# Projections of two sequences together in the last attention of an eight-layer kernel, and inverse square roots by bits and Newton's steps

## The chip, the core and the metric

The kernel runs on one core of a Trainium2 chip. A core has five engines, each with its own instruction queue worked off in order: TensorE (PE, matmuls, with weight loads shown as PEld), VectorE (DVE), ScalarE (ACT), GpSimd (POOL) and SyncE (SP, which only starts transfers). They meet through semaphores. The metric is the device time of one execution in microseconds. The kernel before took 2527.54 us, the median of three runs between 2524.89 and 2529.49.

## The reference

Eight sequences of 256 tokens with 256 features go through eight layers, an attention and a feed-forward in turn, four times; after each layer the input is added and a layer norm follows. The change lies in the seventh layer (a differential attention) and in the very last norm of the eighth (a mixture of 32 experts, four per token). Cut to what matters:

```python
def L3_attn(x):                        # 16 heads, 4 key/value heads, D = 16
    q = rope(x @ Wq); k = rope(x @ Wk); v = x @ Wv
    scores = softmax(causal(q k^T / sqrt(D)))        # two maps per head
    diff = softmax(causal(scores[0] - lam * scores[1]))
    att = diff @ v
    att = att * rsqrt(mean(att * att, -1) + 1e-8) * rms_w
    return (att * (1 - lam_init)) @ Wo

x = layernorm(x + L3_attn(x))
x = layernorm(x + L3_ffn(x))           # softmax over 32 experts, top 4
```

A layer norm here is (x - mean) / sqrt(var + 1e-5).

## The kernel before, in words

The tokens stay on chip: X[b] holds sequence b with tokens on the partitions, xT[k] holds blocks of two sequences transposed (512 columns), which is what matmuls need. PSUM is eight banks of 128x512 f32, handed out by `ps(tag)`: two each for the tags t, a, s and o, in turn.

`attn3` (from L553) is software-pipelined by hand. Within it the order on PE, DVE, ACT and POOL is exactly the order in which the Python code issues instructions; no planner moves them. SP's order is planned by the framework, in this stage and in the next. A **unit** is one sequence b, one half qc of its queries (128 of them) and a group of heads: for qc = 0 there are two units of 128 keys with four score maps each per slot, for qc = 1 four units of 256 keys with two maps. So a sequence has six units, and the loop at the end of `attn3` runs 48 + 3 rounds. I call the rounds of a sequence r0 to r5; r0 and r1 have a unit with qc = 0. Round n does, in this order:

- `factors` of unit n-1: a reciprocal of the softmax sums (DVE, L672), then on POOL a causal select, the factor c in two small products (L682, L683), and another select
- `scores` of unit n: matmuls into four banks, two a and two s (PE, L642), a masking matmul (L655), then row maxima (DVE, L659), then exponentials with sums (ACT, L662)
- `values` of unit n-3: matmuls of the probabilities with V into a bank of tag o (L739), and when a half is complete a copy to oS (L118 or L120, DVE and ACT in turn)
- one step of the projection of the next sequence, then the first half of `differences` of unit n-1: the differences (DVE, L696), their maximum (L700), and on POOL a small product (L701) and the shifted differences v (L704)
- one more projection step (two in r0 and r1), then one step of `finish` of an earlier sequence (the queue `ends`)
- the second half of `differences`
- `turned` of unit n-2: transposes on PE into two banks of tag t (L721), then exponentials on ACT (L723)

A **projection step** (`project`, L596 and L600) is two matmuls of 256 columns into a bank of tag t and a DVE multiplication by a rotary table out of it; twelve of them make q and k of one sequence, and a thirteenth makes V (L616, copied out at L620). All of sequence 0 is projected ahead of the loop.

**finish** (L749 on) normalizes a sequence in six steps: transposes of oS, division by the softmax sums and squares; mean squares (L773) and their inverse root by Ln and Exp on ACT (L780, L781) and one Newton step on POOL (L782 to L785), then the scaling of att (L788); transposes (L795) and a copy aT (L799); the output matmul (L804), the residual (L164) and `moments`; the normed rows; and the transposes for the next layer. Its steps begin in r3 of the following sequence, one per round.

`moments` (L176) takes means and variances on DVE and calls `rsqrt` (L141), which computes (var + eps) to the power -0.5 with two POOL instructions (L146, L147).

When sequence 3 is finished, the sort of the first group of tokens for the experts starts between the rounds (the queue `others`), and then POOL issues 32 indirect transfers that scatter the tokens to sorted rows (L954), three per round.

`ffn3` then runs the expert tiles of group 0, between which the rest of `attn3` (the finish of sequence 7) and the sort of group 1 are stepped; then the tiles of group 1; then `ffn3_combine` of group 1: per half sequence POOL issues four indirect gathers (L2048), DVE adds them up weighted (L2054), and after two halves `moments`, the norm and the output transfer (L197) follow.

Of the kernel before, what the change touches and what calls it, by code (L numbers as in the profile page):

```python
# [10 lines left out]
F32 = mybir.dt.float32  # L11
# [28 lines left out]
class Model:  # L40
# [135 lines left out]
    def moments(self, r):  # L176
# [8 lines left out]
        self.rsqrt(rstd, mv[:, :, 1], 1.0, LN_EPS)  # L185
# [367 lines left out]
    def attn3(self, w, act, keep, start=False, beside=None):  # L553
# [29 lines left out]
        qTs, kTs, oT, oSs = {}, {}, {}, {}  # L583

        def project(b):

            if start:
                self.transpose_x(b)
            xT = self.xT[b // 2][:, :, (b % 2) * T : (b % 2 + 1) * T]
            qT = act.tile([P, 8, T], F32, tag="qT", name="qT")  # L590
            kT = act.tile([P, 2, T], F32, tag="kT", name="kT")

            def turn(out, wt, i, tab):
                ps = self.ps("t")[:, :T]
                for c in range(2):
                    nc.tensor.matmul(  # L596
                        ps, wt[:, c, i * P : (i + 1) * P], xT[:, c, :],
                        start=(c == 0), stop=(c == 1),
                    )
                nc.vector.tensor_tensor(out, ps, tab, ALU.mult)  # L600

            for a in range(2):
                k = kT[:, a, :]
                turn(k, w["wk"], 2 * a, w["ck"][:, a, :])
                yield
                x = act.tile([P, T], F32, tag="kh", name="kh", bufs=1)
                turn(x, w["wk"], 2 * a + 1, w["sk"][:, a, :])
                nc.gpsimd.tensor_tensor(k, k, x, ALU.add)
                yield
            for j in range(8):  # L610
                turn(qT[:, j, :], w["wq"], j, w["tq"][:, j % 2, :])
                yield
            ps = self.ps("t")[:, :128].rearrange("p (t n) -> p t n", t=2)
            for t in range(2):
                for c in range(2):
                    nc.tensor.matmul(  # L616
                        ps[:, t, :], xT[:, c, t * P : (t + 1) * P], w["wv"][:, c, :],
                        start=(c == 0), stop=(c == 1),
                    )
            nc.vector.tensor_copy(  # L620
                Vs[b % 2][:, :, :, 0:16], ps.rearrange("p t (s d) -> p t s d", s=4)
            )
            qTs[b], kTs[b] = qT, kT
            yield
# [1668 lines left out]
```

## Time and profile before

| what | us |
|---|---|
| median of three runs | 2527.54 |
| profiled execution, its own time | 2512.97 |
| its span | 2511.2 |
| setup and projections of sequence 0 | 1741 to 1759 |
| rounds of attn3 | 1759 to 2216 |
| expert tiles of group 0 | 2216 to 2346 |
| expert tiles of group 1 | 2346 to 2455 |
| gathers and last norms | 2455 to 2511 |

Over the whole span PE is busy 2192.5 us (87%), DVE 1431.1 (57%), ACT 1047.5 (42%) and POOL 916.9 (37%). These shares are means over stages with different limits. Where a stretch of the trace is listed, each row has busy time and number of instructions of each engine in it, then the mean granted TensorE clock, the share of time in which the transfer engines were busy, and GB/s. A list of waits names the waiting engine, tile and line, then the releasing one, the total in us, how often, and the longest. In a timeline an idle time stands in brackets with the instruction that ended it. Successive DVE instructions overlap a little: a 128x512 instruction that shows 0.68 lets the next start after 0.60, a 128x256 one that shows 0.41 after 0.33.

### The profile page before, as it was taken

What the parts mean: (1) busy time and instruction counts of PE and PEld (TensorE: products, weight loads), DVE (VectorE), ACT (ScalarE), POOL (GpSimd) and SP (SyncE); (2) the same over time, 40 slices, a digit from 0 to 9 for tenths busy, and PEclk for the clock granted to TensorE, in tenths of its full rate; (3) what the DMA queues carried; (4) which work ended last, traced back from release to release, by engine and by line L of the source; (5) the groups of instructions that cost most, each with busy time, mean ns of one, the idle gap of its engine ahead of it and who ended that gap; (6) DMA issues with size and microseconds to landing.
All of it is one profiled execution on the core that took longest, in us unless ns stands there. A gap on an engine that the chain in (4) does not pass through costs nothing. (4 is left out here: it accounts for less than half of the span.)

```text
span 2511.2 us, 36255 instructions
## 1 busy us (share of the span) xinstructions
PE 2192.5 (87%) x11960; PEld 1494.2 (60%) x12016; DVE 1431.1 (57%) x3593; ACT 1047.5 (42%) x3005; POOL 916.9 (37%) x1725
## 2 busy tenths in 40 slices
PE   7998899999999999999999999998877777678990
PEld 4554697756666666666664465555555554457780
DVE  4556486754544543544465454565888878645463
ACT  1334365453544544544432112221766755644450
POOL 1222443343433323333312321000566557833555
PEclk9999999999999999999999999999999978789995
DMA  5000411100000100000260011002000000145663
GB/s 160 1 1 1 165 44 40 59 5 4 3 3 8 47 1 1 1 1 1 74 206 1 1 51 52 1 0 103 1 2 1 1 1 26 41 125 172 213 212 96
DMA packets 92309, 120.76 MB, mean 48 GB/s; under 512 B 9757, under 2 KB 79582, under 8 KB 91102
## 3 DMA queue, kind: packets, MB, share of 16 engines
q1 hardware_dynamic: 82270, 95.75, 11.8%
q0 software_dynamic: 8192, 21.11, 2.8%
q8 instruction: 100, 1.64, 0.3%
q10 hardware_dynamic: 1664, 1.57, 0.2%
q14 instruction: 83, 0.68, 0.1%
HBM read 67.53 MB, written 50.88 MB: 47 GB/s over the span
## 5 line engine op out<-in xcount | busy, mean ns | idle before, releaser
L1391 POOL TENSOR_SCALAR p<-p,rs 128x128 f32<-128x128 f32 (+1 forms) x256 | 104.2, 425 | 294.7 <-DVE rs L1389 290.4
L1381 ACT ACTIVATE p<-ps_s,nm,rq 128x128 f32<-128x128 f32 (+1 forms) x256 | 128.0, 507 | 152.2 <-DVE nm L1379 152.2
L1309 ACT ACTIVATE sq<-ps_a 128x512 f32<-128x512 f32 x126 | 76.0, 603 | 227.2 <-PE ps_a L1301 226.9
L146 POOL TENSOR_SCALAR rsq<-bnmv 128x2 f32<-128x2 f32 x64 | 13.6, 212 | 377.5 <-DVE bnmv L184 369.9
L662 ACT ACTIVATE e<-ps_a,nm 128x128 f32<-128x128 f32 (+1 forms) x256 | 105.9, 435 | 107.7 <-DVE nm L659 98.4
L1310 DVE TENSOR_REDUCE ssk<-sq 128x4 f32<-128x512 f32 x64 | 43.8, 686 | 172.9 <-ACT sq L1309 172.9
L704 POOL TENSOR_SCALAR v<-e,r,nmd 128x128 f32<-128x128 f32 (+1 forms) x256 | 134.6, 537 | 10.0
L1301 PE MATMUL ps_a<-w_a_wq,xT 128*128 128x512 f32 x256 | 122.3, 600 | 12.4 <-DVE k L1323 9.4
L721 PE MATMUL ps_t<-ident,v 128*128 128x128 f32 x384 | 69.2, 317 | 61.7 <-DVE qT L600 29.4
L1301 PE MATMUL ps_a<-w_a_wv,xT 128*128 128x512 f32 x256 | 120.6, 593 | 1.0 <-ACT q L1334 1.0
L1981 PE MATMUL ps_a<-w_f_gup,xTg 128*128 x504 | 111.5, 345 | 11.4 <-DVE xTg L1975 6.9
L696 DVE SCALAR_TENSOR_TENSOR e<-e,c 128x128 f32<-128x128 f32 (+1 forms) x256 | 105.1, 460 | 25.5 <-POOL c L683 25.3
L1310 DVE TENSOR_REDUCE ssq<-sq 128x4 f32<-128x512 f32 x64 | 43.9, 686 | 129.8 <-ACT sq L1309 129.8
L1301 PE MATMUL ps_a<-w_a_wk,xT 128*128 128x512 f32 x248 | 116.5, 593 | 0.0
L1429 PE MATMUL ps_o<-w_a_wo,attT 128*128 128x256 f32 x512 | 111.8, 379 | 0.0
L662 ACT ACTIVATE e<-ps_s,nm 128x128 f32<-128x128 f32 (+1 forms) x256 | 106.8, 452 | 0.0
L1429 PEld LDWEIGHTS ps_o<-w_a_wo,attT 128*128 128x128 f32 x512 | 96.7, 190 | 12.8
L1163 DVE SCALAR_TENSOR_TENSOR yg<-ps_t,xg,yg 128x128 f32<-128x128 f32 x266 | 93.1, 350 | 12.7 <-PE ps_t L1152 3.9
L1368 PE MATMUL ps_s<-kT,qT 128*128 128x256 f32 (+1 forms) x512 | 100.3, 329 | 0.0
L721 PEld LDWEIGHTS ps_t<-ident,v 128*128 128x128 f32 x384 | 50.2, 163 | 81.4 <-issue 31.4
L1415 PE MATMUL ps_o<-pT,V 128*128 128x256 f32 x256 | 79.5, 392 | 19.2 <-ACT pT L120 19.2
L1981 PEld LDWEIGHTS ps_a<-w_f_gup,xTg 128*128 128x128 f32 x504 | 82.4, 197 | 22.2 <-ACT yg L2011 10.6
(410 smaller groups left out, 6041.7 us busy)
## 6 DMA issues: line engine op xcount, KB each, us to landing
rows<-zero SPq DMA_DIRECT2D x42, 384.0 KB, 4.5
xg<-rows SPq DMA_DIRECT2D x42, 384.0 KB, 5.1
outs<-yg SPq DMA_DIRECT2D x42, 384.0 KB, 3.7
w_f_gup<-in_f_gup SPq DMA_DIRECT2D x8, 768.0 KB, 8.6
w_f_w<-in_f_w SPq DMA_DIRECT2D x8, 512.0 KB, 6.3
w_f_down<-in_f_down SPq DMA_DIRECT2D x8, 384.0 KB, 8.3
w_f_up<-in_f_up SPq DMA_DIRECT2D x5, 512.0 KB, 7.3
lrows<-zero SPq DMA_DIRECT2D x12, 204.0 KB, 5.7
```

The source lines that it names most:

```text
L662: nc.scalar.activation(e[:, s, j * nk : (j + 1) * nk], sc[s][:, j, :], AF.Exp, bias=nm[:, s, j : j + 1], scale=1.0, accum_out=sums[:, s, j ...
L696: nc.vector.scalar_tensor_tensor(d[:, s, h, :], u.e[:, s, h, 1, :], u.c[:, s, h : h + 1], d[:, s, h, :], ALU.mult, ALU.add,)
L704: nc.gpsimd.tensor_scalar(u.v[:, s, h, :], d[:, s, h, :], u.r[:, s, h, 0:1], nm[:, s, h : h + 1], ALU.mult, ALU.add,)
L721: nc.tensor.transpose(ps[:, s, c, :], x, self.ident)
L1163: nc.vector.scalar_tensor_tensor(acc[j], y, c, acc[j], ALU.mult, ALU.add)
L1301: nc.tensor.matmul(ps, self.xt(u.b, t, c), w[which][:, c, u.cols], start=(c == 0), stop=(c == 1),)
L1310: nc.vector.tensor_reduce(out, sq, AX.X, ALU.add)
L1368: nc.tensor.matmul(sc[:, j, :], u.qT[:, h0 + j, qc * P : (qc + 1) * P], u.kT[:, h0 + j, 0:nk], start=(j == 0), stop=False,)
L1381: nc.scalar.activation(u.p[qc][:, h0 + j, :], sc[:, j, :], AF.Exp, bias=nm[:, j : j + 1], scale=r[:, j : j + 1], accum_out=u.sums[qc][:, h ...
L1391: nc.gpsimd.tensor_scalar(u.p[qc][:, j, :], u.p[qc][:, j, :], ri[:, j : j + 1], 1.0, ALU.mult, ALU.mult,)
L1429: nc.tensor.matmul(y[:, t, :], attTs[b][:, h, t * P : (t + 1) * P], w["wo"][:, h, :], start=(h == 0), stop=(h == 15),)
L1981: nc.tensor.matmul(ps, xT[j][:, c, :], w["gup"][:, bass.ds(er[j], 1), c, :].rearrange("p o f -> p (o f)"), start=(c == 0), stop=(c == 1),)
```

## The change

In `attn3`:

- Projections are made for a block of two sequences, so a part has 512 columns instead of 256, and there are twelve parts per block. Block 0 (sequences 0 and 1) is projected ahead of the loop; the parts of block k + 1 are issued one per round in the twelve rounds of block k. The two banks of tag o are taken once: `bank_o` for the values, `bank_x` for the parts and for V. The DVE instruction that empties a part comes at the start of the next round, ahead of the row maxima. V is still made per sequence, in r2, and the part of r2 follows at the end of that round.
- The shifted differences v are written over the differences in e instead of to a tile of their own; qT becomes four tiles per block.
- The inverse root in `finish`: two DVE instructions make a first guess from the bits, one more forms the mean, and three Newton steps of four POOL instructions each replace the Ln, the Exp and the one Newton step.
- `finish` has twelve steps instead of six, and two are taken per round, so that it still lasts six rounds.

In `ffn3`: the leftover of `attn3` is stepped at two of three tiles instead of one of three; and the norms of group 1, except the last, take their root by bits and Newton's steps on DVE instead of POOL's power.

```diff
+    def rsqrt_bits(self, out, v, eng):
+        half = ... tag="nm" ...
+        self.nc.vector.tensor_scalar(half, v.bitcast(I32), 1, None, ALU.arith_shift_right)
+        self.nc.vector.tensor_scalar(
+            out.bitcast(I32), half, -1.0, float(0x5F3759DF), ALU.mult, ALU.add)
+        for _ in range(3):
+            eng.tensor_tensor(t, out, out, ALU.mult)
+            eng.tensor_tensor(t, t, v, ALU.mult)
+            eng.tensor_scalar(t, t, -0.5, 1.5, ALU.mult, ALU.add)
+            eng.tensor_tensor(out, out, t, ALU.mult)
...
+        bank_o, bank_x = self.ps("o"), self.ps("o")
+        def project(blk, banks):
+            def part(to, wt, i, tab):
+                def turn():
+                    ps.append(banks())
+                    for c in range(2):
+                        nc.tensor.matmul(ps[0], wt[:, c, i * P : (i + 1) * P], xT[:, c, :], ...)
+                def out():
+                    nc.vector.tensor_tensor(to..., ps[0]..., tab..., ALU.mult)
+                    if wt is w["wk"] and i % 2:
+                        nc.gpsimd.tensor_tensor(k, k, to, ALU.add)
...
-                u.v = act.tile([P, 4, u.nh, u.nk], F32, tag="v", name="v", bufs=3)
+                u.v = d
...
             yield
+            yield
             ms = self.small.tile([P, 2, 16], F32, tag="ms", name="ms")
...
-            g.tensor_scalar(ms, ms, 1.0 / 16.0, 1e-8, ALU.mult, ALU.add)
+            nc.vector.tensor_scalar(ms, ms, 1.0 / 16.0, 1e-8, ALU.mult, ALU.add)
+            nc.vector.tensor_scalar(half, ms.bitcast(I32), 1, None, ALU.arith_shift_right)
-            nc.scalar.activation(rr, ms, AF.Ln)
-            nc.scalar.activation(rr, rr, AF.Exp, scale=-0.5)
-            g.tensor_tensor(ms, ms, rr, ALU.mult)
-            g.tensor_tensor(ms, ms, rr, ALU.mult)
-            g.tensor_scalar(ms, ms, -0.5, 1.5, ALU.mult, ALU.add)
-            g.tensor_tensor(rr, rr, ms, ALU.mult)
+            nc.vector.tensor_scalar(
+                rr.bitcast(I32), half, -1.0, float(0x5F3759DF), ALU.mult, ALU.add)
+            yield
+            for i in range(3):
+                g.tensor_tensor(t, rr, rr, ALU.mult)
+                g.tensor_tensor(t, t, ms, ALU.mult)
+                g.tensor_scalar(t, t, -0.5, 1.5, ALU.mult, ALU.add)
+                g.tensor_tensor(rr, rr, t, ALU.mult)
+                if i < 2:
+                    yield
...
+            if out:
+                out()
...
-            step(projections)
+            v = project_v(n // 6 + 1) if n % 6 == 2 and n // 6 + 1 < NB else None
+            if v:
+                v[0]()
+            elif parts:
+                f, out = parts.pop(0)
+                f()
             halves = last.differences() if last else iter(())
             next(halves, None)
-            step(projections, 2 if u and u.qc == 0 else 1)
             step(ends)
+            if v:
+                v[1]()
...
+            step(ends)
+            if v and parts:
+                f, out = parts.pop(0)
+                f()
...
-                m = self.moments(rs[b])
+                m = self.moments(rs[b], g == 1 and i < 2 * n - 1)
...
-            if len(left) > 1 and j % 3 != 2:
+            if len(left) > 1 and j % 3 == 0:
```

## The prediction

> **What bounds the kernel now.** I read the busy times by stretch first, one row per sequence of the seventh layer (1854 to 1907 is sequence 2).
>
> ```profile
> core 0: us, PE busy (x) PEld busy (x) DVE busy (x) ACT busy (x) POOL busy (x), PEclk, DMA share, GB/s
> 1741.00:1759.00 18.00, 17.00 (x98) 13.92 (x99) 7.39 (x20) 0.59 (x1) 2.05 (x3) 0.81 0.80 326
> ...
> 1854.00:1907.00 53.00, 40.18 (x369) 27.54 (x360) 45.31 (x102) 37.46 (x147) 33.51 (x83) 0.97 0.01 1
> 1907.00:1961.00 54.00, 42.73 (x364) 29.15 (x360) 45.60 (x103) 37.05 (x146) 33.29 (x81) 0.91 0.00 1
> ...
> 2146.00:2216.00 70.00, 46.81 (x346) 28.75 (x346) 46.98 (x105) 39.70 (x151) 55.37 (x115) 0.76 0.10 35
> ...
> 2455.00:2511.00 56.00, 0.00 (x0) 0.00 (x0) 22.24 (x56) 0.00 (x0) 34.80 (x40) 0.50 0.32 94
> ```
>
> In sequences 2 to 4 DVE is busy 45 of 53 us: it is the bound, with 8 us of stalls. In sequence 7 POOL has taken over, because it also issues the scatter. In the tail only POOL and DVE work. The list of waits (1760 to 2200) names the stalls.
>
> ```profile
> POOL nmd L701 <- DVE nmd L700: 91.0, 53, 8.1
> ...
> PE ps_t L721 <- DVE qT L600: 29.4, 23, 3.1
> ...
> DVE e L696 <- POOL c L683: 16.8, 14, 2.9
> DVE nm L659 <- PE ps_a L655: 16.8, 17, 2.3
> ...
> POOL ms L782 <- ACT rr L781: 13.7, 7, 2.0
> ...
> DVE V L620 <- PE ps_t L616: 11.9, 6, 5.2
> ...
> DVE res L164 <- PE ps_t L804: 8.8, 5, 1.8
> ```
>
> The largest is harmless: POOL waits for the engine that bounds. The fourth to the last are what DVE itself loses. PE waits for DVE to empty t banks and so starts the next scores late (29.4, then 16.8 for DVE). POOL waits for ACT's root and then gives c late. The timeline shows this in r4 and r5 of sequence 2, ACT first:
>
> ```profile
> 1895.45 1.28 ACT L780 ACT_TABLE_LOAD   x1
> ...
> 1901.33 0.29 DVE L620 COPY V<-ps_t 128x128 f32<-128x128 f32 x1 [1.43 <-PE ps_t L616]
> 1903.48 1.04 DVE L696 SCALAR_TENSOR_TENSOR e<-e,c 128x256 f32<-128x256 f32 x2 [1.86 <-POOL c L683]
> ```
>
> Two table loads and two small activations (3.0 us) delay ACT's exponentials, hence the values, V and c: DVE loses 1.43 + 1.86 us. The tail's timeline shows POOL's queue:
>
> ```profile
> 2467.90 0.94 POOL L2048 DMA_INDIRECT yk<-outs,r_slots  x1 [0.30 <-issue]
> 2469.14 0.94 POOL L2048 DMA_INDIRECT yk<-outs,r_slots  x1 [0.30 <-issue]
> 2470.16 0.19 POOL L146 TENSOR_SCALAR rsq<-bnmv 128x2 f32<-128x2 f32 x1
> 2470.43 0.72 POOL L147 TENSOR_TENSOR rstd<-rsq,nhalf 128x2 f32<-128x2 f32 x1
> 2471.34 1.17 POOL L2048 DMA_INDIRECT yk<-outs,r_slots  x1 [0.19 <-issue]
> ```
>
> **Ahead of the loop.** A part of 256 columns takes 0.865 us once the clock is up (DVE empties one each 0.86 us), twelve 10.4; the observed twelve took 13.0, since the first four came at up to 1.7 us. The clock's 2.6 us extra is what must be scaled or not. The row alone suggests doubling all: +13.0. The Trainium skill (TensorE: Matmul & The Clock Gate, Part 1) says that the warm-up is a span of time of about 3.4 us and not a number of matmuls; then only 12 x 0.865 doubles: **+10.4 us**. I take that; the four slow parts fill one such span and a bit. DVE's emptying (0.60 each) is hidden behind PE's 1.73. If that cover failed, it would cost 12 x 0.6 more.
>
> **Rounds of a full sequence.** I add DVE's work between one round's first maximum and the next's, by the starts of the rows: maxima 4 x 0.60 = 2.4; differences and maximum 2.95 for a qc = 1 unit, 3.8 for qc = 0; reciprocal 0.11 or 0.16; a part 0.60 (the 128x512 residual out of a t bank, L164, shows 0.69 and occupies 0.60), so six per sequence cost 3.6 where twelve at 0.33 cost 4.0.
>
> - r0: 2.4 + 2.95 + 0.16 + 0.6 = 6.1, plus a wait for POOL. A Newton instruction is priced by L782 to L785 (0.22 to 0.25, next start 0.33 later), so a step is 1.3. At the end of r5 POOL does step 2 (1.3), the product and v of the second half (1.4), step 3 (1.3) and the scaling (1.2), all behind the first half's v; it ends 5.1 after DVE's last maximum. The select and c (0.9) follow, at 6.0, while DVE needs c after 3.1. DVE waits 2.9: r0 is 9.0.
> - r1: 2.4 + 3.8 + residual and moments 1.8 + normed rows 0.7 + 0.76 = 9.5. Behind scores on PE stand values 0.6, part 1.73 and output matmul 1.73, 4.1 in all; DVE asks at 4.3, so no wait.
> - r2: DVE 7.7. PE is longer: V must be copied out (5.5), the X transposes free a t bank at about 5.6, turned ends at 6.2, the part moved to the end takes 1.73, the scores 1.3: 9.2.
> - r3: 2.4 + 2.95 + divisions 1.2 + 0.7 = 7.3; turned waits for both t banks: 7.4.
> - r4: 2.4 + 0.3 + 2.95 + mean squares 0.65 + three small DVE instructions at 0.2 (a 128x32 integer one, L901, shows 0.18) + 0.7 = 7.6.
> - r5: 6.1 plus 0.5, because POOL's step 1 brings c at 3.6 instead of 3.1: 6.6.
>
> The sum is 49.3. Before, sequences 2, 3 and 4 took 52.9, 54.1 and 53.4 by their first reciprocals. So -4.2 each, **-12.5 us**. The gain is in r5 (9.3 to 6.6) and r3; r1 and r2 get longer (8.4 to 9.5, 8.5 to 9.2). For c and Newton's steps the unknown is POOL's pace: without any waits in r0 and r5 a sequence saves 7.6, with steps at twice the price nothing (below).
>
> **The other sequences.** Sequence 1 took 49.8; without the residual and X transposes in its first rounds r0, r1 and r2 follow the cycle exponentials 5.5, scores 1.5, first maximum 0.7, signals (7.85, 7.85, 8.2), then as above: 45.5, **-4.3**. Sequence 0 has no finish: the first wait for scores now covers the part, **-2**. Sequence 5 holds the sort, whose work stays; -3.6 by the same rounds. In 6 and 7 POOL is the bound: a qc = 0 round with scatter is 9.6, qc = 1 8.1. Newton's twelve instructions (4.0) take the place of five plus the 1.95 wait for ACT (3.6), and the sum of the two k additions (1.5) leaves sequence 6. Table loads no longer delay V (5.2 once) and c. **-2.5 and -2**. In the drain and the expert tiles the finish of sequence 7 takes tiles 1 to 17 instead of 2 to 17: nothing. Its table loads (2229.7 to 2234.1) lay inside a 6.9 us PE wait for a transfer. SP's queue has as many transfers; the gathers of rows and the stores of outs swap places here and there, priced 0, within 3 either way: around 2347 PE waits 3.6 us behind such a store. v in e costs nothing: e is read by turned two rounds later and written again three rounds later, so that cover holds by one PE queue position.
>
> **The tail.** 32 gathers at a cadence of 1.25 us take 38.8 from first start to last; observed are 42.5, so three roots cost 1.23 each. They leave POOL; the last stays. DVE gets fifteen dependent small instructions, about 0.19 each as L184 (0.18): 2.9 in place of the 2.64 wait. Per eight gathers (10 us) DVE has 8 x 0.51 + 1.25 + 2.9 + 0.7 = 9.0, so POOL still sets the end. Against it speaks the skill (GPSIMD Engine Reference, Key points): POOL shares SBUF interfaces with DVE and collides with instructions of two SBUF inputs, of which each root has nine. By the row, gathers beside L2054 (also two inputs) still take 0.94 to 0.95; only those starting with the normed rows (2471.34) show 1.17. By the rule nine gathers would lose 0.22, 2.0 us; by the row none. I take 0.7: -3.7 + 0.7 = **-3**.
>
> **Sum.** 10.4 - 2 - 4.3 - 12.5 - 3.6 - 2.5 - 2 - 3 = -19.5. The profiled execution, 2512.97 with 1.8 outside its span, becomes 2493. The median before lies 14.6 above it; the same difference on it gives 2527.5 - 19.5 = **2508 us**.
>
> **Rivals.**
>
> - *Newton's steps hold up c (slower).* Place: r4, r5 and r0, where twelve POOL instructions stand in the queue ahead of select and c. Small POOL rows do stretch beside DVE: L701 0.19 to 0.36, L146 0.19 to 0.33. At twice the price a step is 2.6; r5 waits 1.3 longer and r0, with two steps behind it, 2.6 to 3. That is 4.2 per sequence, the whole gain of sequences 1 to 5 (-20.4 + 21). The sum is +10.4 - 2 + 0.6 - 4.5 - 3 = +1.5, and with 4.0 us more POOL work in each of the two scattering sequences +9.5: 2537. It decides from about 0.65 us per instruction pitch. Against: the eight of L785 have a median of 0.25, though the longest took 0.52.
> - *DVE closes up fully.* If c and the scores are never late, sequences 1 to 5 fall to DVE's 45 to 46 us, 3 to 4 less than I said: -35 in all, 2492. For it: POOL is idle a third of the time. Against: in-order queues, and PE's r2.
> - *Nothing is recovered.* If the cycle of exponentials, scores and maxima sets the rounds anyway, 8 a round leaves 48 to 53, and the longer start eats the tail's saving and more: 2515 to 2527. Against: r4 at 7.1 in sequence 2.
>
> **How the numbers follow.** Main case 0.58, 2497 to 2520; DVE closing up 0.16; nothing recovered 0.09; c held up 0.17. A measurement can tell about 0.2%, 5 us: faster is below 2522.5. The first two cases are faster (0.74); the third splits between faster and same; the fourth is slower or nearly so. Faster 0.75, same 0.09, slower 0.16. The range must keep the closing-up case's near half and the near edge of the slow case: 2489 to 2532.
>
> **What would show it.** First maximum about 10 us later after the first projection matmul; no ACT table load between rounds; no PE wait of turned for the emptying of a part; sequences 2 to 4 at 48 to 51 us, r0 with a DVE wait for c of 2 to 3; sequence 7 unchanged; gathers every 1.25 us without gaps except before the last root. It would be wrong if POOL's Newton pitch exceeded 0.5, if the start grew by more than 13, or if PE's clock fell in the rounds, since scores are on the cycle.

## The result, and the profile after

The changed kernel took 2548.38 us (median of six runs, 2544.61 to 2551.78), the kernel before 2524.88 beside it (six runs, 2520.69 to 2529.49): a ratio of 1.009 with a 95% interval of 1.0075 to 1.0106. It is 23.5 us, 0.9%, slower, where 2508 was predicted and nothing above 2532 expected.

One thing is needed to read the numbers that follow. The same program takes different times in different sets of runs: the kernel before took 2522 to 2526 in three sets and 2513 in three others. Where the chip is on record, it goes with the chip (4 and 2 for the first kind; 12 and 6, twice, for the second), so I speak of chips of the first and second kind; but each set ran on one chip, so chip and occasion can't be told apart. The profiled execution of the kernel before (2512.97) is of the second kind, that of the changed kernel (2549.25) of the first, so the two traces may not be subtracted stage by stage. The changed kernel was therefore profiled again on a chip of the second kind. There it took 2524.09 beside 2512.73 for the kernel before (1.0042, 1.0027 to 1.0056): 11.4 us slower. About half of the 23.5 us comes with the change on both kinds of chip; the other half appears only on chips of the first kind.

The traces differ in one more thing. Those of the first kind have lost records. For the same program the first trace of the changed kernel holds 15,003 semaphore events and the second 17,394, and more than half of the missing ones are arrivals of transfers in the expert tiles and the tail. It shows in the lists of transfers, where the last number, the time to arrival, is missing (first kind, then second):

```profile
xg<-rows SPq DMA_DIRECT2D x42, 384.0 KB
...
xg<-rows SPq DMA_DIRECT2D x42, 384.0 KB, 5.0
```

All nine traces of the first kind are like that and none of the eleven of the second. Every execution here was recorded, so whether the recording itself slows chips of the first kind is not known.

The busy times by stretch of the changed kernel, in its first trace: start, sequences 2 to 4, sequence 7 with the drain, tail. Columns as in the rows shown of the kernel before.

```profile
core 0: us, PE busy (x) PEld busy (x) DVE busy (x) ACT busy (x) POOL busy (x), PEclk, DMA share, GB/s
1746.00:1776.00 30.00, 27.73 (x102) 13.55 (x102) 11.33 (x18) 5.27 (x28) 3.17 (x3) 0.96 0.41 167
1865.00:1921.00 56.00, 44.31 (x326) 25.99 (x332) 45.55 (x98) 34.09 (x143) 35.00 (x89) 0.82 0.00 1
1921.00:1973.00 52.00, 40.49 (x352) 24.68 (x347) 44.91 (x100) 33.70 (x143) 32.87 (x87) 0.97 0.01 1
1973.00:2030.00 57.00, 44.58 (x332) 25.95 (x332) 45.91 (x99) 34.30 (x144) 35.54 (x89) 0.85 0.00 1
2147.00:2227.00 80.00, 48.95 (x366) 30.17 (x368) 51.18 (x112) 40.42 (x163) 65.76 (x145) 0.70 0.10 34
2475.00:2547.00 72.00, 2.45 (x10) 1.19 (x9) 30.25 (x102) 2.15 (x7) 31.68 (x35) 0.53 0.28 84
```

Sequences 2 to 4 take 56.5, 52.0 and 57.1 us by their first reciprocals; they took 52.9, 54.1 and 53.4. DVE has the same 45 us of work, so it stalls for 7 to 11 us where it stalled for 8. In sequences 2 and 4 TensorE's clock fell to 0.82 and 0.85 (0.97 and 0.88 before). The list of waits (1760 to 2212) shows which stalls there are now:

```profile
engine line waited for: us in total, times, longest us
...
DVE e L742 <- POOL c L729: 27.8, 18, 5.7
...
DVE nm L705 <- PE ps_a L701: 15.0, 13, 1.9
...
PE ps_t L767 <- DVE att L805: 13.5, 7, 3.5
PE ps_t L848 <- POOL att L841: 12.1, 6, 4.8
...
DVE nm L705 <- remote: 11.2, 7, 3.1
PE ps_t L767 <- DVE xT L118: 10.8, 3, 3.9
...
PE ps_t L767 <- ACT aT L852: 8.9, 5, 3.2
...
DVE kT L632 <- PE ps_o L626: 6.8, 3, 2.6
```

The transposes of the probabilities no longer wait for the emptying of a part (29.4 us before), as intended. In its place PE waits for att to be scaled on POOL, for the copies aT and xT, and for the divisions. DVE waits longer for c than before (22.9 us up to 2205; the list shown with the prediction ends at 2200, just ahead of a wait of 6.1, and has 16.8), and for scores ("remote" are scores whose releaser the profile does not name).

The terms of the prediction's sum, from the two profiles that can be compared, the changed kernel's second (span 2524.4) and that of before (2511.2), by the first and last instruction of each stretch:

| stretch | predicted | measured |
|---|---|---|
| setup (to the first projection matmul) | 0 | +3.2 |
| start (from there to the first reciprocal) | +10.4 | 30.7 - 21.8 = +8.9 |
| sequences 2 to 4 | -12.5 | 165.4 - 160.4 = +5.0 |
| the other sequences | -14.4 | 271.2 - 278.5 = -7.3 |
| drain (last reciprocal to first expert matmul) | 0 | 20.1 - 15.0 = +5.1 |
| expert tiles | 0 | 230.9 - 229.3 = +1.6 |
| tail | -3 | 59.4 - 62.7 = -3.3 |
| sum | -19.5 | +13.2 |

The setup's 3.2 is not the change's alone: versions with unchanged setup and old projections began their first projection at 1742.9 to 1744.1, those with the new ones at 1742.2 to 1746.7. What moves it is open. It also shortens the next row. TensorE's granted clock was 0.50 up to 1748.5 in the trace of before, 5.0 us behind its first projection matmul, and up to 1749.0 in that of the changed kernel, only 2.3 us behind (two rows of before, then two of the changed kernel's second trace):

```profile
1743.50:1748.40 4.90, 4.90 (x12) 3.91 (x13) 0.85 (x2) 0.35 (x1) 0.58 (x1) 0.50 1.01 416
1748.60:1765.00 16.40, 14.47 (x98) 11.67 (x97) 8.12 (x18) 5.42 (x32) 2.05 (x3) 1.00 0.40 164
...
1746.70:1748.90 2.20, 2.20 (x3) 1.16 (x4) 0.00 (x0) 0.34 (x1) 0.00 (x0) 0.50 0.99 402
1749.10:1776.00 26.90, 24.98 (x97) 12.05 (x96) 11.08 (x17) 4.29 (x25) 3.18 (x3) 1.00 0.35 145
```

In six other versions with the same twelve parts it stayed at 0.50 for 4.9 to 5.1 us behind that matmul, as in before, and the start took 32.1 us: +10.3.

Of the -7.3 in the other sequences -6.3 falls in sequence 6 alone (61.6 to 55.3), where -2.5 was predicted. Sequences 0, 1, 5 and 7 together gave 1.0 of the 11.9 us predicted for them.

### The profile page after: what moved, and what is told of

Same layout as the page of the kernel before. It is cut to its first block, busy times and chain, and to the rows that moved or that the text cites. A ratio compares the mean times of both kernels' runs of the same rounds, so it can differ in the third digit from the quotient of the medians.

```text
span 2547.5 us, 35930 instructions
## 1 busy us (share of the span) xinstructions
PE 2211.9 (87%) x11769; PEld 1471.6 (58%) x11824; DVE 1436.4 (56%) x3614; ACT 1019.1 (40%) x2972; POOL 921.4 (36%) x1767
## 5 line engine op out<-in xcount | busy, mean ns | idle before, releaser
L750 POOL TENSOR_SCALAR e<-e,r,nmd 128x128 f32<-128x128 f32 (+1 forms) x256 | 131.0, 523 | 10.0
L767 PE MATMUL ps_t<-ident,e 128*128 128x128 f32 x384 | 66.3, 311 | 53.3 <-DVE att L805 13.5
L767 PEld LDWEIGHTS ps_t<-ident,e 128*128 128x128 f32 x384 | 50.6, 161 | 75.0 <-issue 32.3
```

The costliest lines, as they stand in the source:

```text
L750: nc.gpsimd.tensor_scalar(u.v[:, s, h, :], d[:, s, h, :], u.r[:, s, h, 0:1], nm[:, s, h : h + 1], ALU.mult, ALU.add,)
L767: nc.tensor.transpose(ps[:, s, c, :], x, self.ident)
```

## Experiments on the tail

In the first profile of the changed kernel the gathers follow each other without a gap every 1.25 us, as predicted, and yet the tail takes 72.9 us, 10 more than before. The timeline of DVE in the second root:

```profile
2504.75 0.30 DVE L202 TENSOR_SCALAR rsv<-bnmv 128x2 f32<-128x2 f32 x1
2505.17 0.17 DVE L180 TENSOR_SCALAR rsh<-rsv 128x2 int32<-128x2 int32 x1
2505.87 0.17 DVE L181 TENSOR_SCALAR rstd<-rsh 128x2 int32<-128x2 int32 x1 [0.53 <-DVE rsh L180]
2506.60 0.20 DVE L186 TENSOR_TENSOR rst<-rstd 128x2 f32<-128x2 f32 x1 [0.56 <-DVE rstd L181]
2507.30 0.16 DVE L187 TENSOR_TENSOR rst<-rst,rsv 128x2 f32<-128x2 f32 x1 [0.50 <-DVE rst L186]
2508.01 0.17 DVE L188 TENSOR_SCALAR rst<-rst 128x2 f32<-128x2 f32 x1 [0.55 <-issue]
```

An instruction of 0.17 us starts every 0.70 us, later mostly every 1.40, as if on a grid. The root lasts 15.2 us where the first and the third take 3.3 and 3.0. The grid begins 24 us after the first gather and ends 6 us after the last one has started; the sums (L2131) in it are slowed too. It is in all seven traces of the first kind whose second root is by bits.

**The bit roots alone** (the kernel before with `rsqrt_bits` in the last norms, as below) and **all but the bit roots** (the changed kernel with the old line):

```diff
-                m = self.moments(rs[b])
+                m = self.moments(rs[b], g == 1 and i < 2 * n - 1)
```

> The kernel before with only the roots of the last norms by bits and Newton's steps on DVE; attention and pacing as before. Theory A (in the tail of the changed kernel DVE lost 12 us in one root to a pause that depends on where in DVE's instruction stream the root falls, not on the roots themselves): here the roots fall elsewhere, each takes about 3.3 us, gathers run every 1.25 us, the tail from the last expert matmul to the end takes 59 to 60 us where it took 62.7, and the time is 3 us below before, 2522. Theory B (short dependent DVE instructions beside POOL's gathers are slow as such): at least one root takes about 15 us again, the tail 70 to 73, the time 2533 to 2537.

> The changed kernel with the power on POOL in all the last norms, as before; all else changed. Theory A and B alike: the 10 us of the tail come back, 62 to 64 us from the last expert matmul to the end, and the time is 2538 to 2540. Rival C (the tail is late for another reason, such as gathers that start later against the tiles): the tail stays above 68 and the time within 4 us of 2548.

Alone they took 2528.63 beside 2522.11 (1.0028, 1.0018 to 1.0039), with a tail of 71.8 us and the grid in the second root. Without them the changed kernel took 2535.77 (1.005, 1.0033 to 1.0068), with a tail of 62.8. So the roots make the tail's loss, on this chip (of the first kind), whatever stands before them.

**DVE's stream shifted.** Theory A was that the root falls on a place in DVE's stream where instructions are being fetched.

```diff
+        for _ in range(64):
+            self.nc.vector.memset(idle, 0.0)
```

> The changed kernel with 64 memsets of one column on DVE in a pause of the start (9 to 14 us of the execution, where DVE waits for the first projections), which move every later DVE instruction 64 places down its stream and change nothing else. Theory A (the pause of 0.70 us per instruction in the second root of the tail hangs on the place in DVE's stream, as when its instructions are being fetched while the gathers run): the three roots take about 3.3 us each, the tail 58 to 60 us, the time 2536 to 2539. Theory B (contention of the root's instructions with POOL's gathers): the second root takes about 15 us again and the time is 2547 to 2550.

It took 2543.86 (1.0088, 1.0071 to 1.0106), with a tail of 72.0 and the grid again in the second root. Theory A falls, for this shift.

**Gathers that wait for no sum.** Gathers 17 to 32 reuse the four yk tiles, so each waits on DVE. In the kernel with the bit roots alone they were given the xT tiles instead.

```diff
+                if g == 1 and t >= 4:
+                    ys[t] = self.xT[t - 4].rearrange("p c (h d) -> p (c h) d", h=2)
```

> The kernel before with the bit roots of the last norms, as in the run with these alone (2528.6, tail 71.8), and the gathers of the second half of the tail written to four tiles of their own (the xT tiles, free by then) instead of the four used by the first half, so that no gather waits for a DVE sum. Theory F (the second root is slow because gathers 17 to 32 wait on the semaphore on which DVE's own chain of small instructions waits): all three roots take about 3.3 us, the tail 58 to 60 us, and the time is 2515 to 2520, below before. Theory B (DVE's dependent instructions are slowed by a long gap-free row of gathers as such, from about 24 us after the first): the second root takes 12 us or more again, the tail stays at 70 to 73 and the time at 2526 to 2531.

It took 2536.24 beside 2525.75 (1.0038, 1.0024 to 1.0052), and the grid was there again: the second root ran from 2492 to 2509. The gathers' waits are not the cause.

**The second root on POOL**, and **POOL's gaps kept** (bit roots on DVE, and the old power beside them into a tile nobody reads):

```diff
-                m = self.moments(rs[b])
+                m = self.moments(rs[b], g == 1 and i in (1, 5))
```

> The kernel before with bit roots on DVE in the first and third of the last norms only; the second stays a power on POOL. Theory J (a row of small dependent instructions on DVE is slow only in the later half of the gathers, from about 24 us after the first to 5 us behind the last): both bit roots take 3.3 us, one gap of 1.2 us is left among the gathers, the tail from the last expert matmul is 60 to 61 us where before had 62.7, and the time is 2 us below before, not to be told from it. Rival K (any DVE work is slow there, the sums too, once POOL's gathers run nearly without gaps): the second block's sums take over 5 us longer and the tail is 66 or more.

```diff
...
+            self.rsqrt_bits(rstd, v, nc.vector)
+            idle = self.small.tile([P, 2], F32, tag="idle", name="idle")
+            self.rsqrt(idle, mv[:, :, 1], 1.0, LN_EPS)
```

> The kernel before with the bit roots on DVE and, beside them, the old power on POOL into a tile that nobody reads, so that POOL's gathers have their gaps of 1.2 us after each block as before. Theory L (the pause needs gathers without a gap): all three roots 3.3 us, tail 62 to 64, the time within 2 us of before. Theory J (the small DVE instructions late in the gathers are enough): the second root again 10 us or more, the tail 68 to 74, the time 5 to 10 above before.

The first took 2510.82 beside 2513.35 (0.9992, 0.9984 to 1.0001), tail 60.6; the second 2512.77 (0.9997, 0.9989 to 1.0006), tail 62.6, three undisturbed roots. But these runs decide nothing between theories J, K and L: they fell on a chip of the second kind, and a kernel run beside them with three bit roots and gathers without gaps (below) had no grid either, and a tail of 59.3.

**The changed kernel once more.**

> The changed kernel itself once more, with a profile. Theory Q (the pause in the second root, and 8 to 12 us of the expert tiles, belong to the chip on which a run falls: they were there where the kernel before took 2522 to 2526 and absent, in the same instructions, where it took 2513): on a chip of the first kind the tail is 71 to 73, the tiles 238 to 242, and the time 23 above before; on one of the second kind the tail is 59 to 60, the tiles 229 to 231, and the time 9 to 12 above before. Theory R (the pause belongs to the program): tail 71 to 73 and 23 us above before on any chip.

2524.09 beside 2512.73, tail 59.4, tiles 230.9: theory Q, on each of its numbers for a chip of the second kind, and theory R falls. The same program, the same second root, gathers again every 1.25 us:

```profile
2495.17 0.30 DVE L202 TENSOR_SCALAR rsv<-bnmv 128x2 f32<-128x2 f32 x1
2495.51 0.17 DVE L180 TENSOR_SCALAR rsh<-rsv 128x2 int32<-128x2 int32 x1
2495.71 0.17 DVE L181 TENSOR_SCALAR rstd<-rsh 128x2 int32<-128x2 int32 x1
2495.92 0.16 DVE L186 TENSOR_TENSOR rst<-rstd 128x2 f32<-128x2 f32 x1
2496.11 0.16 DVE L187 TENSOR_TENSOR rst<-rst,rsv 128x2 f32<-128x2 f32 x1
2496.31 0.42 DVE L188 TENSOR_SCALAR rst<-rst 128x2 f32<-128x2 f32 x1
```

A start every 0.20 us. The expert tiles differ by chip in the same way, without the change: with old projections and old finish they took 237 and 242 us on chips of the first kind and 228 to 229 on chips of the second. What slows a chip of the first kind there is open. Neither the place in the stream nor the gathers' waits is it; whether gaps between the gathers avoid it was not tried on such a chip. The rival that stands untested is the recording. For it: more than half of the missing records are missing in these two stretches. Against it: some 480 arrivals are missing between 250 and 500 us as well, and the first projection, at 1746.3 us beside 1746.7, is not later for it.

## Experiments on the pace, the start and the rounds

**The old pace of the leftover.**

```diff
-            if len(left) > 1 and j % 3 == 0:
+            if len(left) > 1 and j % 3 != 2:
```

> The changed kernel with the leftover of the attention stepped at one of three expert tiles, as before, instead of two of three. Theory D (the 11.7 us that the expert tiles gained come from the pace: the second sort and the rest of the finish press on the tiles): the stretch of expert tiles falls from 239.9 to 229 to 234, the time to 2537 to 2543. Rival E (the tiles are slow for another reason, a lower clock or a place in the instruction stream, or vary from run to run): the stretch stays at 236 or more and the time within 4 us of 2548.

2563.49 (1.0167, 1.0148 to 1.0186), tiles 255.3 us: both theories missed: the tiles got longer, where one expected them shorter and the other unchanged. With twelve steps at one in three tiles the second sort ends so late that PE stands still before the second group ("PE ps_t L2050 <- DMA xg<-rows: 23.2, 1, 23.2"). The new pace belongs to the longer finish; with it the tiles take 1.6 us more than before (table above).

**The finish alone** (old projections, old norms), and **the projections alone**. The second kernel also has the new roots of the last norms; its tail (73.8) is left out of the reading.

```diff
+            step(ends)
...
-            nc.scalar.activation(rr, ms, AF.Ln)
-            nc.scalar.activation(rr, rr, AF.Exp, scale=-0.5)
...
+            nc.vector.tensor_scalar(half, ms.bitcast(I32), 1, None, ALU.arith_shift_right)
...
+            for i in range(3):
+                t = keep.tile([P, 2, 16], F32, tag="rt", name="rt", bufs=1)
+                g.tensor_tensor(t, rr, rr, ALU.mult)
...
```

> The kernel before with only the new finish: root by bits and Newton's steps, twelve steps, two per round, leftover stepped at two of three tiles; old projections and old last norms. If the prediction's account of the rounds holds (table loads cost V and c 1.9 to 3.3 us per sequence, Newton's steps cost r0 some of it): sequences 2 to 4 at 51 to 53 us, the drain 2 to 5 us longer, the time 2512 to 2522. If c in r0 and the later end of the finish eat it: sequences at 53 to 55, drain 5 longer, the time 2525 to 2535.

> The kernel before with only the new projections (two sequences together, bank of their own, a part a round), old finish with table loads in six steps, old last norms, old pace. Prediction's account: start 9 to 10 longer, one sequence 1 to 3 us shorter, so the time 2522 to 2530. Rival (a part of 512 columns beside the emptying of V in the same bank puts PE on the path, and what twelve DVE emptyings save is lost): sequences 2 to 4 at 53 to 57, the time 2530 to 2538, that is nearly all of the 13.7 us that the changed kernel loses without its last norms.

The finish alone took 2540.75 beside 2525.75 (1.0061, 1.0044 to 1.0078). Its rounds took 448.7 us (438.9 before), sequences 2 to 4 57.8, 57.4 and 57.3, outside both of my ranges. The projections took 2536.74 (1.0042, 1.0029 to 1.0054), of which the tail is 11: rounds 433.5, sequences 2 to 4 53.3 to 54.1, start 32.1 instead of 21.8. So the projections gain 5 us in the rounds, about half of what their start costs (10), and the finish, for which the gain of r5 was claimed, loses 10. Three things qualify this. The projections' gain isn't in sequences 2 to 4 (161.0 us in all, 160.4 before) but in sequence 6 (61.6 to 56.0). The attention of the kernel before, unchanged, took 435.8 to 439.1 in the rounds of four other runs, so 5 is 2 to 5. And the two don't add up: together they make -2.4, not +4, so each changes what the other costs. DVE in the finish alone, in r1 of sequence 2:

```profile
1865.65 0.69 DVE L659 TENSOR_REDUCE nm<-ps_a 128x4 f32<-128x512 f32 x1 [3.12 <-remote]
1873.12 0.69 DVE L164 TENSOR_TENSOR res<-ps_t,X 128x512 f32<-128x512 f32 x1 [1.75 <-PE ps_t L814]
```

The scores are 3.1 us late, the output matmul 1.8. The same two waits in the changed kernel (its line numbers are others):

```profile
1876.72 0.69 DVE L705 TENSOR_REDUCE nm<-ps_a 128x4 f32<-128x512 f32 x1 [1.27 <-remote]
...
1882.38 0.69 DVE L164 TENSOR_TENSOR res<-ps_t,X 128x512 f32<-128x512 f32 x1 [1.41 <-PE ps_t L858]
```

There the chain to the late scores can be read from PE's timeline (r0 and the beginning of r1 of sequence 2):

```profile
1870.12 1.02 PE L848 MATMUL ps_t<-ident,att 128*128 128x128 f32 x4 [1.67 <-POOL att L841]
1873.00 1.11 PE L767 MATMUL ps_t<-ident,e 128*128 128x128 f32 x4 [1.43 <-ACT aT L852]
```

PE waits for the scaling of att, then, for its transposes of the probabilities, for the t bank that the copy aT holds; aT stands on ACT behind the exponentials of r0's unit. All that PE has behind that, the next scores first, is late. In the kernel before these transposes came in r5; the twelve-step finish moves them to r0.

**The root a round earlier**: two Newton steps instead of three, both in r4, the scaling in r5.

```diff
-            yield
-            for i in range(3):
+            for i in range(2):
...
-                if i < 2:
-                    yield
+                yield
```

> The changed kernel with two Newton steps instead of three, both a round earlier (with the first guess and right after it), and the scaling in the round after; PE's transposes and all later steps stay where they are. Theory M (POOL's Newton steps and scaling stand in front of c, 3.0 us per sequence, and end too late for PE's transposes of att, so that the next scores are late, 1.3 us, and the drain is 4.5 us longer): sequences 2 to 4, 51 to 57 before this edit, fall to 49 to 53, the drain from 20 to 16 or 17, and the time by 10 to 18, to 2530 to 2538. Rival N (PE and the exponentials set the rounds whatever POOL does): sequences stay at 52 to 57, the time within 5 us of 2548.

2522.13 beside 2513.35 (1.0034, 1.002 to 1.0047), 8.8 above before where the changed kernel is 11.4 above on such a chip: a gain of 2.6, not 10 to 18. (The times expected here, and below for the shorter start's first version, were counted from a chip of the first kind; only the distance to before can be compared.) The drain fell from 20.1 to 16.7, as theory M says. The rounds did not: 436.9 us. DVE's wait for c went (10.9 us to 3.6 in 1800 to 2030), and a wait for scores took its place (4.3 us named and 5.6 "remote" in the changed kernel):

```profile
engine line waited for: us in total, times, longest us
...
DVE nm L705 <- PE ps_a L701: 16.4, 9, 3.5
PE ps_t L767 <- ACT aT L851: 11.2, 3, 3.8
...
DVE e L742 <- POOL c L729: 3.6, 7, 0.6
```

In the changed kernel DVE reached r1 late because of c, and found the scores nearly ready. Take c away and it waits for them: r0 fell from 9.3 to 7.2 us, and r1 grew from between 11.0 and 12.3 to between 13.3 and 14.6.

**The copy aT on DVE**, with the earlier root:

```diff
-            nc.scalar.copy(aT, pt)
+            nc.vector.tensor_copy(aT, pt)
```

> The kernel with the earlier two-step root, and the copy aT of the transposed att on DVE instead of ACT. Theory P (in the round of the first unit of a sequence this copy stands behind that unit's exponentials on ACT and holds a t bank; PE's transposes of the probabilities wait for it up to 3.8 us, the next scores are late, and DVE waits 3.4 us for them): the round after it falls from 13.3 to 14.6 to 10 to 11, sequences 2 to 4 from 55 to 57 to 51 to 54, the rounds in all 15 to 20 shorter, the time 5 to 12 below before where the version with the copy on ACT was 8.8 above. Rival S (the exponentials themselves bound these rounds): sequences stay at 54 or more and the time within 4 of 8.8 above before.

2514.17 beside 2512.73 (1.0003, 0.9994 to 1.0012), 1.4 above before. The rounds fell by 6.3 us to 430.7, r1 to 11.3 to 11.7, sequences to 54.5, 52.3 and 53.8. Theory P names a real cause, but it is worth a third of what I gave it.

**The copy xT on ACT.** In the changed kernel this copy alternates between DVE and ACT. Where it falls on DVE (sequences 2 and 4), PE waits for it in r2, and the part behind is slow:

```profile
1893.31 1.09 PE L767 MATMUL ps_t<-ident,e 128*128 128x128 f32 x4 [3.18 <-DVE xT L118]
1894.19 3.62 PE L626 MATMUL ps_o<-xT,w_a_wk 128*128 128x512 f32 x4
```

The part of r0 took 1.98 us. It looks as if the pause of 3.18 us had cost PE its clock, and theory G below says so, but the clock fell ahead of the pause, which began at 1890.1:

```profile
core 0: us, PE busy (x) PEld busy (x) DVE busy (x) ACT busy (x) POOL busy (x), PEclk, DMA share, GB/s
1885.12:1888.53 3.41, 2.02 (x30) 1.54 (x28) 3.38 (x9) 0.47 (x3) 2.56 (x7) 1.00 0.01 2
1888.60:1893.30 4.70, 1.53 (x8) 1.15 (x7) 4.67 (x10) 4.18 (x17) 3.04 (x7) 0.50 0.00 0
```

A table of the Trainium skill (TensorE: Matmul & The Clock Gate, Part 1) puts the fall to half rate after an idle window of about 3.4 us. Here it came behind 3.41 us in which PE was busy for 2.02 and its longest pause was 1.39, so no idle window was needed.

```diff
-            self.norm_done(b, last=False)
+            self.transpose_x(b, self.nc.scalar.copy)
```

> The changed kernel with the copy that ends each finish (the transposed X of the next layer) always on ACT instead of on DVE and ACT in turn. Theory G (in every other sequence this copy falls on DVE behind the differences, PE's transposes of the probabilities wait 3.2 us for its bank, the clock falls and the part behind takes 3.6 us instead of 2.0): sequences 2 and 4, 56 to 57 us, fall to 52 to 54 like sequence 3, the part of r2 takes 2 us in all, the time falls by 5 to 9, to 2539 to 2543. Rival (the copy on ACT delays the exponentials by as much): sequences stay at 55 to 57 and the time within 4 us of 2548.

2550.05 (1.0094, 1.0077 to 1.0111), nothing gained. Sequences took 56.2, 54.9 and 54.2. PE now waits at the same place for POOL's shifted differences, and the clock fell at 1888.7, again ahead of the wait:

```profile
1893.13 1.09 PE L767 MATMUL ps_t<-ident,e 128*128 128x128 f32 x4 [2.73 <-POOL nmd L747]
1894.01 3.62 PE L626 MATMUL ps_o<-xT,w_a_wk 128*128 128x512 f32 x4
```

With the copy on ACT in all three sequences, r2 + r3 took 19.9, 19.5 and 18.8 us at mean clocks of 0.74, 0.83 and 0.91. In the changed kernel's sequence 3, where the copy is on ACT too, they took 16.7 at 1.00. In these rounds the loss goes with the clock, whichever engine makes the copy.

**A shorter start.** Only eight of block 0's parts ahead of the loop, the other four behind the scores of the first unit; first with the earlier root, then also with aT on DVE. Both have the second of the last roots on POOL.

```diff
+        rest, ahead = ahead[8:], ahead[:8]
...
+            for f, g in rest:
+                f()
+                g()
```

> The changed kernel with the earlier two-step root, with only eight of block 0's twelve parts ahead of the loop (the other four behind the first unit's scores), and with the second of the last roots on POOL. If the three repairs add up: 10 to 18 by the rounds and the drain, 3 by the start, 12 by the tail, so 2515 to 2523, at or a little below before. If only the tail's holds: 2534 to 2538.

> The same with eight of the twelve parts of block 0 ahead of the loop and the second of the last roots on POOL. If theory P holds and the start gives back 3 to 5: 8 to 16 below before. By rival S: 2 to 6 above.

2518.71 beside 2513.35 (1.0025, 1.0014 to 1.0036) and 2510.34 beside 2512.73 (0.9992, 0.9985 to 0.9999). The start took 26.9 us, where twelve parts ahead of the loop took 30.7 to 32.1. The first was expected at or a little below before and is 5.4 above. The second is the best version with the new projections, 2.4 us below before: less than 0.2%, and no more than the kernel before gains by two bit roots alone (2510.82 beside 2513.35).

**The old projections** with the earlier root, aT on DVE and two bit roots at the end: the kernel before with the finish of the version above, two steps of it per round.

```diff
+            step(ends)
...
-            nc.scalar.copy(aT, pt)
+            nc.vector.tensor_copy(aT, pt)
...
-            if len(left) > 1 and j % 3 != 2:
+            if len(left) > 1 and j % 3 == 0:
```

> The kernel before with its own projections, the finish with the earlier two-step root, aT on DVE, two steps a round, leftover at two of three tiles, and bit roots in the first and third of the last norms. If the start's cost of the new projections is the larger part and theory P holds here too: no table loads, sequences 2 to 4 at 50 to 53, the time 5 to 15 below before, and so below the version with new projections. If PE's waits for emptied parts keep the rounds as they were: within 4 of before.

2512.99 (0.9997, 0.9988 to 1.0006). Rounds 438.6, as before; the tail gives 2.2 and the drain takes 2.1. Theory P does not hold here.

**Parts moved to light rounds**: none in r1 and behind V, two in r4 and in r5; or one only, from behind V to r5.

```diff
-            elif parts:
+            elif parts and n % 6 not in (1,):
...
+            if n % 6 in (4, 5) and out:
+                out()
...
-            if v and parts:
-                f, out = parts.pop(0)
-                f()
+            if n % 6 in (4, 5) and parts:
+                f, out = parts.pop(0)
+                f()
```

> The version with earlier root, aT on DVE and split start, and the block's parts moved: none in r1, none behind the V of r2, two each in r4 and r5 (the first emptied between the halves of the differences, the second issued before the transposes of the probabilities). Theory T (r3 is 11.5 because DVE waits 2.6 us for the part issued at the end of r2 by a PE that waited for a t bank and lost its clock; r1 is 11.7 since PE's queue holds scores, part and output matmul): r3 falls to 8 to 9, r1 to 10 to 11, r4 and r5 grow by 0.6 to 1.2 each, sequences 2 to 4 to 50 to 53 from 54, and the time is 10 to 20 below before. Rival S (the wait moves to r4 and r5 or to the next scores): sequences stay at 53 to 55 and the time within 5 of 2.4 below before.

> The same version with one part moved only, from behind V at the end of r2 to r5 as a second part; r1 keeps its part. Theory T: r3 falls by 2.5 to 3.5, r5 grows by 0.6 to 1.2, r1 stays, sequences at 52 to 53, the time 8 to 14 below before. Rival S: within 5 of 2.4 below before.

2526.1 beside 2512.8 (1.0061, 1.0043 to 1.0079) and 2514.27 (1.0006, 0.9997 to 1.0015). In the first r3 fell to 8.0 to 8.4 us and r1 to 10.0 (11.4 to 12.0 and 11.7 before the edit), but r5 grew from 6.8 to between 10.7 and 12.0, and r0 from 7.7 to between 9.2 and 10.9; rival S has the place, but neither foresaw a loss of 13 us. With one part moved r3 fell from 11.4 us to 8.1, as theory T says. But r0 grew from 7.7 to 10.9 and r5 from 6.8 to 8.6, and the sequence is as long as it was (54.2; 54.4 before the edit). DVE's waits from r2 to r0, first without the move, then with it:

```profile
1889.51 0.69 DVE L632 TENSOR_TENSOR kT<-ps_o,w_c_ck 128x512 f32<-128x512 f32 x1 [2.58 <-PE ps_o L626]
1891.02 0.69 DVE L705 TENSOR_REDUCE nm<-ps_a 128x2 f32<-128x512 f32 x1 [0.82 <-PE ps_a L701]
...
1916.98 1.01 DVE L742 SCALAR_TENSOR_TENSOR e<-e,c 128x256 f32<-128x256 f32 x2 [0.58 <-POOL c L729]
```

```profile
1890.79 0.69 DVE L705 TENSOR_REDUCE nm<-ps_a 128x2 f32<-128x512 f32 x1 [0.80 <-PE ps_a L701]
...
1915.99 0.69 DVE L632 TENSOR_TENSOR qT<-ps_o,w_c_tq 128x512 f32<-128x512 f32 x1 [1.75 <-PE ps_o L626]
1918.48 0.69 DVE L705 TENSOR_REDUCE nm<-ps_a 128x4 f32<-128x512 f32 x1 [1.80 <-PE ps_t L767]
```

The 2.58 us for the part are gone and 1.75 + 1.80 have come. Rival S holds: the wait moves.

## Why the prediction was wrong

It failed at one step, the **rounds of a full sequence**, and at one cover, the **drain**. On traces that can be compared, forecast and measurement lie 32.7 us apart: 24.6 of them are the rounds, 5.1 the drain, 3.2 the setup and 1.6 the tiles, less 1.8 in the start and the tail. On chips of the first kind the grid adds 13.5 us to the tail (72.9 beside 59.4), for which the sum had no term.

- *Ahead of the loop*, +10.4: right. At the same stretch of half clock as before it was +10.3; the +8.9 of the table has 1.4 of luck in it, because a later setup left only 2.3 us of half clock for the first parts. The row alone would have said +13.0, and the page's rule (TensorE: Matmul & The Clock Gate: the warm-up is a span of time, not a number of matmuls) was the right choice. Where the page says about 3.4 us, the half clock lasted 5.0 us behind the first matmul in the trace of before.
- *The rounds*, -26.9 in all: wrong, -2.3, of which sequence 6 makes -6.3. Some of the terms were right: r5 6.75 for 6.6 and r0 9.32 for 9.0, with DVE waits for c of 0.46 and 3.0 for 0.5 and 2.9. Newton's instructions started every 0.30 to 0.35 us, as priced. The terms that failed are "r1 ... no wait" (9.5; 11.1 to 12.3 measured), r2 + r3 (16.6; 16.7 in sequence 3, 20.2 and 20.4 in 2 and 4) and, by less, r4 (7.6; 8.2 to 8.3). For r1 I added PE's queue behind the scores, but took the scores themselves to be on time. They were not: PE had waited in r0 for att and for aT. I had priced where POOL's scaling ends for DVE's c, and not for PE's transposes, which stand in the queue ahead of the next scores. For r2 and r3 I took PE to be at its full clock: in sequence 3 it was (1.00), and the sum came out; in 2 and 4 it was 0.75 and 0.83. That the clock could fall in the rounds was named among the signs of being wrong, but no price was put on it. How the waits and the clock share the loss between them is not shown, since PE's pauses come ahead of the fall and a slow PE makes the next wait longer.
- Behind all of them is one assumption: that a DVE stall that goes is gained. Seven versions of the changed kernel took one or two waits out of the rounds, and each time another took most of it up or all: c by scores, xT by POOL, the part's in r3 by two in r0. DVE's 45 us of work were never the length of a sequence, and no version brought one of sequences 2 to 4 below 51.9 us. Of the rivals, "nothing is recovered" (0.09) described the rounds, though the cycle of exponentials that it gives as the reason was not tested; the argument against it (r4 at 7.1 us in one sequence) was of one round and said nothing of the ring of six.
- *The drain*, "nothing": wrong, +5.1. The finish that begins in the last round now reaches its transposes a round later, and PE waits for POOL there: "PE L848 MATMUL ps_t<-ident,att ... [6.25 <-POOL att L841]" at 2217.92. With the root a round earlier that wait was 2.83 and the drain 3.4 shorter, so this cause is shown for 3.4 of the 5.1.
- *The tail*, -3: right where no grid appears (-3.3). Of the row and the page that were weighed, the row was right: gathers beside the roots' two-input instructions took 0.94 to 0.95 us. (The page is GPSIMD Engine Reference of the Trainium skill, Key points.) On chips of the first kind the term was +10, by an effect that the trace of before could not show.
- *The rival "Newton's steps hold up c"*, on the slow side, was not what happened. The result is slower, but by scores, the drain and the tail.
- The time itself was set on the median of the runs shown, 14.6 us above the profiled execution, as if that difference were noise. The runs were of the first kind and the profile of the second, and on the first kind this change costs 12 us more.

## What to carry to other kernels

When an in-order pipeline turns over several engines, a stall removed on the busiest one is an upper bound and not a gain. Follow the step that you move through every queue it stands in (here PE's transposes and ACT's copy, not only POOL's arithmetic), and ask in which round its copy now stands behind which exponentials. When a wait is followed by a lower clock, look when the clock fell: it can have fallen first. A profile whose time lies outside the range of its kernel's runs is a profile of other conditions: compare traces only when the reference beside them took the same time.

## What the runs showed of the hardware

- In runs on chips of the first kind DVE started small dependent instructions mostly 0.70 us or a multiple of it apart, from 24 to 26 us into a row of indirect gathers until about 6 us behind the start of the last; on chips of the second kind the same instructions started every 0.20 us. The cause is open, and the traces of the first kind have lost records (15,003 semaphore events for 17,394), more than half of the missing ones there and in the expert tiles.
- The expert tiles, with gathers and transfers beside them, take 237 to 242 us on the first chips and 227 to 231 on the others, at the same granted clock of the whole execution (0.94 to 0.95).
- PE's granted clock fell to 0.50 behind 3.41 us in which PE was busy for 2.02 with no pause above 1.39; a part took 3.62 us instead of 1.98.
- At the start the clock was 0.50 for 4.9 to 5.1 us behind the first projection matmul in six traces with twelve parts ahead of the loop, and for 2.3 in three; the stretch up to the first reciprocal then took 32.1 and 30.7 us.
